# Two routed tiles of 128 rows moved into the last attention steps of a transformer block, with the order of output adds and weight transfers changed

## The chip, the cores and the metric

The kernel runs on one core of a Trainium2 chip. The metric is device time in microseconds (us). TensorE (PE) does the matmuls, VectorE (DVE) and ScalarE (ACT) the element-wise work, GpSimd (POOL) indirect transfers and some arithmetic, SyncE (SP) issues most transfers. Everything is in float32, where a matmul is done as two instructions on TensorE; 256 columns take 2 x 0.216 us.

## The reference

```python
x = x + attn(cond(x, cond_8, ...), ...)
x = x + ffn(cond2(x, cond_8, ...), ...)
# B, S, D = 4, 512, 256
# cond:  one of 8 gated MLPs (256 -> 512 -> 256) for each sequence, silu(up) * gate
# attn:  16 query heads of 16, one shared key/value head, softmax over 512 keys
# cond2: weights mixed from 8 matrices per sequence, masked: x @ w + bias
# ffn:   8 groups of 256 tokens, router with 8 experts, the top 2 chosen by each token,
#        at most 128 tokens of a group for one expert:
h = gelu_tanh(einsum('gech,ehf->gecf', expert_in, wi))     # 256 -> 1024
expert_out = einsum('gecf,efh->gech', h, wo)               # 1024 -> 256
out = einsum('gech,gtec->gth', expert_out, combine)        # combine = probability * dispatch
```

## The kernel before

**Attention.** There are 16 units (4 sequences of 4 units), each of 4 steps; a step is numbered n from -8 to 64 and has four slots i. In a slot the main loop emits the row maxima of eight steps ahead (`maxima`: a matmul into `pm`, L461, and a negated maximum on DVE, L463; none from step 56 on, since there is no unit left), the exponentials (`exponentials`: matmul `pe`, L490, and Exp on ACT, L491), and every second step the product of the weights e with v (`weigh`, 16 narrow matmuls L500 in slot 2). `shifts`, `shift_rows` (L480) carry a unit's maxima through DRAM back into the rows of `qq`.

**Side work.** All other work of the four sequences is cut into pieces. A track holds a list of pieces with a cost each, and a start and an end step; `pump(now)` runs pieces of the track that lags most, until what is due (at most 1100 cost units in a slot) is done. A piece emits matmuls into a bank from `side()`, a PSUM pool of two banks, and returns a `take`, the work on ACT or DVE that empties the bank, which `take_out` runs in the next slot; a take can return a second part for the slot after. A piece that returns OPEN keeps its bank for the next piece of its track. From step 38 (THIN) on, a slot without matmuls of a piece gets a filler, a matmul with zeros (`fill`, L516).

`finish(b)` holds the pieces after attention for sequence b: the output projection (L648), the transposes of r (L684), the mixing matmuls (L696), the router's choices on DVE and the scatter of the rows into `xp`, in one region per expert (`numbered`, L850, indirect transfers from GpSimd). Sequence 3's pieces run in the tail.

**Routed units.** After the rows of two sequences are scattered, the first full pairs of tiles (256 rows of one expert) are known. `full_list` lists them on DVE; `used` counts the pairs taken for each expert. The units are 3 "first", 4 "early" (listed after three sequences), 3 "pair", and 8 "last" with 320 to 96 rows. `fetch_in` and `fetch_out` bring a unit's weights (wi and wo, 1 MB each, three buffers of each) and rows. `up` multiplies (L1170) and applies the activation on ACT (L1174), `put` multiplies again (L1236), scales by the token's probability on DVE (`weights`, L1195 to L1213) and adds the rows to the output in DRAM by an indirect transfer with add (L1216), one for each tile of up to 128 rows. Unused rows point to spare output rows. The tail starts with `up` of the first unit, when the last attention step is emitted, and `go` interleaves up of unit t with put of unit t - 1; `pieces` lists what else is emitted at which chunk, a chunk being a fourth of a 256-row unit's up or put.

**Order of transfers.** SP's and GpSimd's queues run in the order written. The weights of the three first units are issued by GpSimd at steps (59, 2), (61, 1) and (62, 1). The reciprocals of the softmax sums of units 12 and 13 (`inverted`, the transfers `inv_rows<-hl`) are issued by SP at step 59 and used by `normalised` at (62, 1).

Of the kernel before, what the change touches and what calls it, by code (L numbers as in the profile page):

```python
# [32 lines left out]
NPAIR = NT // P  # L33
FIRST = 3
EARLY = 4
# [20 lines left out]
def adaln_attn_ffn_kernel(  # L56
# [154 lines left out]
    spare1 = numbers("spare1", [P, 1], [[0, 1]], NT + 1, 1)  # L211
# [40 lines left out]
    for n in range(4):  # L252
        t = apool.tile([P, 4, T], F32R, name=f"qq{n}")
        nc.gpsimd.memset(t[64:65].bitcast(F32), 0.0)
        qq.append(t)
# [17 lines left out]
    ep = attn_ctx.enter_context(tc.tile_pool(name="ep", bufs=2))  # L273
    scatters, last_rows, adds = [], [], []
# [603 lines left out]
    full_of = {"first": 2, "early": 3}  # L878
# [71 lines left out]

    used = lt("used", [P, NE])
    nc.gpsimd.memset(used, 0.0)

    def behind_used(first):
        nc.vector.scalar_tensor_tensor(
            first[:, 0:NE], used, 2.0 * P, first[:, 0:NE], ALU.mult, ALU.add
        )
        return first


    def full_list(name, n):
        whole = tiles_of(name, ALU.is_ge)

        nc.vector.tensor_scalar(whole, whole, -1.0, None, ALU.add)
        yield
        pairs = pairs_of(name, whole)
        nc.vector.tensor_tensor(pairs, pairs, used, ALU.subtract)
# [13 lines left out]
        nc.vector.tensor_tensor(used, used, end, ALU.add)  # L981
# [6 lines left out]
    def late_lists():  # L988
        count = lt("count", [P, NE])
        nc.vector.tensor_tensor(count, free, base[:, 0:NE], ALU.subtract)  # L990
        c = lt("c_more", [P, NE, 3])
# [4 lines left out]
        nc.vector.tensor_tensor(pairs, pairs, used, ALU.subtract)  # L996
        nc.vector.tensor_scalar(pairs, pairs, 0.0, None, ALU.max)
# [7 lines left out]
        whole = lt("whole", [P, NE])  # L1005
        nc.vector.tensor_tensor(whole, pairs, used, ALU.add)
        rest = lt("rest", [P, NE])
        nc.vector.scalar_tensor_tensor(rest, whole, -2.0 * P, count, ALU.mult, ALU.add)
        at = lt("at_rest", [P, NE])
        nc.vector.scalar_tensor_tensor(at, whole, 2.0 * P, base[:, 0:NE], ALU.mult, ALU.add)  # L1010
# [53 lines left out]
    def routed(units, alone=None):  # L1064
# [8 lines left out]
        def kind(t):  # L1073
            name, n = units[t]
            size = {"last": SIZES[n % NE], "rest": 2 * P + REST}.get(name, 2 * P)
            return lists[name], n, size
# [6 lines left out]
        def queue(t):  # L1083
            return nc.gpsimd if units[t][0] == "first" else nc.sync

        def fetch_in(t, weights=True, tokens=True):
# [23 lines left out]
            if name in full_of:  # L1110
                full = scatters[: 8 * full_of[name]]
                tc.declare_no_dep(
                    i.ins, group="rows", keep=[k.ins for k in full], reason="full tiles"
                )
                tc.add_to_no_dep_group(f"{name} rows", i.ins)
                if n == 0:
                    behind(i, full, "rows of the sequences so far")
            elif units[t] == ("pair", 0):
                behind(i, scatters, "rows of every sequence")

# [58 lines left out]


        def put(t):
            (expert, _), n, size = kind(t)
# [6 lines left out]
            def weights(i, m):  # L1189
                number, e0, p0, p1 = (  # L1190
                    xt_of[t][i][0:m, DX + j : DX + j + 1] for j in range(4)
                )
                w, v = w0[0:m, i : i + 1], w1[0:m, i : i + 1]
                te = expert[0:m, n : n + 1]
                nc.vector.scalar_tensor_tensor(w, e0, te, p0, ALU.is_equal, ALU.mult)  # L1195
                nc.vector.scalar_tensor_tensor(v, e0, te, p1, ALU.not_equal, ALU.mult)  # L1196
                nc.vector.tensor_tensor(w, w, v, ALU.add)
                nc.vector.scalar_tensor_tensor(v, number, 0.0, spare1[0:m], ALU.is_equal, ALU.mult)
                nc.vector.scalar_tensor_tensor(
                    at[0:m, i : i + 1], number, -1.0, v, ALU.add, ALU.add  # L1200
                )

            mine = []
            adds.append(mine)

            def out(i, m, p):
                weights(i, m)
                if m <= REST:
# [11 lines left out]
                    in_offset=None,  # L1220
                    compute_op=ALU.add,
# [3 lines left out]
                elif units[t] == ("pair", 0):  # L1225
                    behind(a, last_rows, "the last sequence's rows")
                mine.append(a)
# [22 lines left out]
            yield  # L1250

# [25 lines left out]
        return ahead, turned, go, turn, fetch_in  # L1277
# [28 lines left out]
    def pump(now):  # L1306
# [3 lines left out]
        due = min(sum(max(0, lag(t)) for t in tracks), 1100)  # L1310
        idle = True
        while due > 0 and any(t[4] for t in tracks):
# [3 lines left out]
            if t[4][0][1] in small_ones:  # L1316
                if now > THIN and loaded[0]:
# [46 lines left out]
    for b in range(B):  # L1364
# [3 lines left out]
        for g in range(NE):  # L1368
# [4 lines left out]
            shut.add((n, i))  # L1373
# [7 lines left out]
    ahead, turned, go, _, fetch_in = routed(units[:-1])  # L1381
    at(-4, 1, lambda: defer(router_bias()))
    first = list_parts(full_list("first", FIRST))
    for k in range(12):
        at(56 + k // 8, k // 2 % 4, first, 1)
    for t in range(FIRST):
        at(*((59, 2), (61, 1), (62, 1))[t], ahead, [t], True, False)
    at(58, 2, ahead, range(FIRST), False, True)
# [5 lines left out]
    for n in range(-LEAD, STEPS + 1):  # L1394
        m = n + LEAD
        for i in range(4):
# [23 lines left out]
            elif pump(n + (i + 1) / 4) or (n % 4, i) == (2, 1):  # L1420
                fill(n, i)
        if n == 36:
# [4 lines left out]
    for t in tracks:  # L1427
# [16 lines left out]
        3: [lambda: inverted(u)], 6: [lambda: fetch_in(FIRST)],  # L1444
# [10 lines left out]
    pieces[chunk + 5] = [lambda: late(99)]  # L1455
    chunks = 0
# [10 lines left out]
    last_ahead, _, last_go, last_turn, _ = routed(units[-1:], alone)  # L1467
# [5 lines left out]
    go(step, then, (FIRST,))  # L1473
# [4 lines left out]
    with tc.If(more > 0):  # L1478
        ahead, _, go, _, _ = routed(
# [83 lines left out]
```

## Time and profile before

| | |
|---|---|
| median of 3 runs | 654.77 us (653.52 to 658.9) |
| the profiled execution: time | 654.26 us |
| its span, first to last instruction | 652.6 us |
| mean granted clock of TensorE | 0.977 |
| PE busy in the span | 614.9 us (94%) |
| DVE, ACT, POOL busy | 340.5, 238.2, 175.8 us |
| moved by DMA | 97.37 MB |
| step 56's `weigh` starts, step 64's | 341.66, 380.83 us |
| the tail's first matmul | 382.69 us |

A chain of waits follows the work that ended last back through what released it. In its lines the first number is the start in us, the second the length. Windows give the busy time of each engine in a stretch; the last three columns are the granted clock of TensorE (1.00 is full), the share in which the DMA engines were busy, and GB/s.

### The profile page before, as it was taken

The numbers are of one execution on the slowest core, as the hardware profiler recorded it, in microseconds if no ns is written. First come the engines' busy times: TensorE is split into PE (matmuls) and PEld (weight loads), VectorE is DVE, ScalarE is ACT, GpSimd is POOL, SyncE is SP. The second block draws the span as 40 slices with busy tenths as digits, with TensorE's granted clock in tenths as the row PEclk, the third lists the DMA queues.
The fourth block names the chain that finished last, engine by engine and source line by source line (L and its number), as shares of the span: only waits on it lengthen the run. The fifth ranks groups of instructions, "written<-read, shape, count | busy, mean of one in ns | idle before, by whom it ended". The sixth has DMA issues, their size and how long they took to land.

```text
span 652.6 us, 8247 instructions
## 1 busy us (share of the span) xinstructions
PE 614.9 (94%) x2821; PEld 404.8 (62%) x2821; DVE 340.5 (52%) x913; ACT 238.2 (36%) x430; POOL 175.8 (27%) x182
## 2 busy tenths in 40 slices
PE   8999899999999999989998499999999999999991
PEld 3445454454455555655454258888889896878880
DVE  3269886668766668988877341247212112122420
ACT  2231556555655555555545341231121112121110
POOL 7008930049000100052024240124321211121231
PEclk9999999999999999999889799999999999999997
DMA  7297375658411242232217824656667777646221
GB/s 241 75 203 267 93 227 154 181 150 251 129 53 50 83 132 54 83 105 96 57 50 255 319 92 158 195 162 188 204 176 208 242 224 194 210 116 223 24 25 20
DMA packets 65876, 97.37 MB, mean 149 GB/s; under 512 B 8290, under 2 KB 37250, under 8 KB 65794
## 3 DMA queue, kind: packets, MB, share of 16 engines
q1 hardware_dynamic: 57826, 81.72, 40.6%
q0 software_dynamic: 8000, 15.04, 9.7%
q8 instruction: 25, 0.41, 0.3%
q14 instruction: 25, 0.20, 0.1%
HBM read 67.24 MB, written 29.24 MB: 148 GB/s over the span
## 4 chain that ended last, share of the span: by engine, by line
PE 79%; DMA 11%; DVE 4%; ACT 3%; issue 1%; POOLq 0%; SPq 0%; DVEq 0%
PE psA L1170 15%; PE psC L1236 14%; PE pa L500 9%; PE pm L461 9%; PE pe L490 9%; PE side L355 7%; DMA out_dram<-y,at 7%; PE side L339 4%; PE side L386 3%; DMA inv_rows<-hl 3%; PE side L648 2%; DVE negm L463 2%; PE side L696 2%; PE pa L516 2%; ACT e L491 2%
## 5 line engine op out<-in xcount | busy, mean ns | idle before, releaser
L491 ACT ACTIVATE e<-pe 128x512 f32<-128x512 f32 x256 | 147.7, 598 | 137.4 <-PE pe L490 133.0
L463 DVE TENSOR_REDUCE negm<-pm 128x1 f32<-128x512 f32 x256 | 167.9, 684 | 55.3 <-PE pm L461 55.0
L461 PE MATMUL pm<-kk,qq 65*128 65x512 f32 x256 | 148.3, 584 | 1.6 <-DVE negm L463 1.5
L1236 PE MATMUL psC<-wo_sb,hT 128*128 128x256 f32 (+2 forms) x544 | 115.4, 381 | 1.0 <-DVE xTr L1147 1.0
L490 PE MATMUL pe<-qq,kk 67*128 67x512 f32 x256 | 108.2, 428 | 2.7 <-ACT e L491 2.2
L1170 PE MATMUL psA<-xTr,wi_sb 128*128 128x256 f32 (+5 forms) x512 | 106.4, 365 | 0.9 <-ACT hT L1174 0.9
L1174 ACT ACTIVATE hT<-psA 128x512 f32<-128x512 f32 (+3 forms) x72 | 38.9, 544 | 183.3 <-PE psA L1170 183.3
L1236 PEld LDWEIGHTS psC<-wo_sb,hT 128*128 128x128 f32 (+2 forms) x544 | 93.2, 182 | 17.3 <-issue 1.7
L1216 POOL DMA_INDIRECT out_dram<-y,at x34 | 52.2, 1536 | 179.0 <-DVE w L1196 67.8
L1170 PEld LDWEIGHTS psA<-xTr,wi_sb 128*128 128x128 f32 x512 | 90.6, 191 | 14.5 <-issue 1.2
L461 PEld LDWEIGHTS pm<-kk,qq 65*128 65x128 f32 x256 | 49.3, 192 | 56.0 <-issue 21.1
L490 PEld LDWEIGHTS pe<-qq,kk 67*128 67x128 f32 x256 | 49.4, 193 | 36.1 <-ACT e L491 26.0
L500 PE MATMUL pa<-e,v 128*32 128x512 f32 x512 | 64.7, 625 | 0.0
L355 PE MATMUL side<-xT_sb,w 128*128 128x512 f32 x128 | 62.2, 595 | 2.2 <-DMA w<-in_wcond_dram 1.4
L1213 DVE TENSOR_SCALAR y<-psC,w 128x256 f32<-128x256 f32 (+1 forms) x30 | 14.4, 481 | 72.1 <-PE psC L1236 72.1
L850 POOL DMA_INDIRECT xp<-x,to_i x32 | 32.9, 1027 | 61.2 <-DVE negm L463 34.2
L1147 DVE COPY xTr<-psC 128x512 f32<-128x512 f32 (+5 forms) x18 | 10.5, 593 | 71.8 <-PE psC L1143 71.8
L577 POOL TENSOR_TENSOR x<-x,bo_sb 128x256 f32<-128x256 f32 x16 | 12.0, 767 | 116.7 <-DMA x<-in_xtok_dram 116.7
L355 PEld LDWEIGHTS side<-xT_sb,w 128*128 128x128 f32 x128 | 24.0, 190 | 18.3 <-issue 9.5
L500 PEld LDWEIGHTS pa<-e,v 128*32 128x32 f32 x512 | 13.9, 113 | 31.7 <-issue 31.1
L339 PE MATMUL side<-hid,w 128*128 128x512 f32 x64 | 31.7, 594 | 0.3 <-DVE hid L321 0.3
L313 DVE SCALAR_TENSOR_TENSOR u<-th,u 128x512 f32<-128x512 f32 x16 | 12.9, 809 | 21.1 <-ACT u L312 21.1
(274 smaller groups left out, 543.6 us busy)
## 6 DMA issues: line engine op xcount, KB each, us to landing
wi_sb<-in_wi_dram SPq DMA_DIRECT2D x14, 1024.0 KB
wo_sb<-in_wo_dram SPq DMA_DIRECT2D x14, 1024.0 KB
xp<-zeros SPq DMA_DIRECT2D x8, 1072.0 KB
qq<-qd SPq DMA_DIRECT2D x32, 256.0 KB
ov<-o SPq DMA_DIRECT2D x16, 256.0 KB
xt<-xp SPq DMA_DIRECT2D x15, 268.0 KB
w<-in_wcond_dram SPq DMA_DIRECT2D x12, 256.0 KB
wi_sb<-in_wi_dram POOLq DMA_DIRECT2D x3, 1024.0 KB, 9.4
```

The lines of the kernel that those rows point to most:

```text
L339: mm(po, wd[:, hc, ts(dc, P)], s["hid"][:, hc, :], start=hc == 0, stop=hc == 3)
L355: mm(s["ps"], s["w"][:, ds(first + P * c, P)], s["xT"][:, c, :], start=c == 0, stop=c == 1,)
L461: mm(pm, qq[u % 4][0:KMAX, hh, ts(i, P)], kk[0:KMAX, :], start=True, stop=True)
L463: nc.vector.tensor_reduce(negm[u % 2][:, c : c + 1], pm, AX.X, ALU.max, negate=True)
L490: mm(pe, kk[0:KEXP, ts(kc, P)], qq[u % 4][0:KEXP, i, :], start=True, stop=True)
L491: nc.scalar.activation(e_of[n][:, i, :], pe, AF.Exp)
L500: mm(pa_of[u][32 * i : 32 * i + 32, :], seqs[u // 4]["v"][:, kc, :], e[:, i], start=False, stop=kc == 3,)
L850: i = nc.gpsimd.indirect_dma_start(out=xp, out_offset=bass.IndirectOffsetOnAxis(ap=to_i[:, k, ch : ch + 1], axis=0), in_=s["x3"][:, ch, :] ...
L1170: mm(ph[:, f, :], of(wi_of[t], c * F + (first + f) * P, P), xT_of[t][:, c, 0:size], start=c == 0, stop=c == 1,)
L1174: nc.scalar.activation(hT_of[t][:, ds(first, per), 0:size], ph, AF.Gelu_apprx_tanh)
L1216: a = nc.gpsimd.indirect_dma_start(out=out_rows, out_offset=bass.IndirectOffsetOnAxis(ap=at[0:m, i : i + 1], axis=0), in_=y[0:m, i, :], in ...
L1236: mm(po[lo : lo + m, i % 2, :], hT_of[t][:, fc, ds(i * P, m)], of(wo_of[t], fc * D, D), start=fc == lo // REST, stop=fc >= F // P - (2 if ...
```

## The change

Two full tiles ("zero", of 128 rows each) are chosen by `zero_list` after the first sequence's rows are known, at steps 43 to 46. `used` counts tiles of 128 rows from now on, not pairs; the later lists subtract it. Their weights are brought by `part_in` in sixteen transfers of 256 KB, one every half step from (46, 2) to (54, 0), on GpSimd's queue. The computation is done by `beside`: nine pieces a tile, in tracks of steps 56 to 60 and 60 to 64. The activation is written out with Square and Tanh on ACT and two operations on DVE. EARLY is 3 instead of 4, so the tail has one unit of 256 rows less.

The adds of one unit's tiles are declared independent of each other and explicitly wait for the unit before; each tile index has spare output rows of its own. The first two units' weights are issued at (58, 0) and (61, 0), the third's by SP in chunk 4 of the tail; the first units' rows come at steps 58, 60 and 62 instead of all at 58. The fetch of unit 3 moves from chunk 6 to 8, the units after the early ones are fetched in two chunks of their own. Two of the four `qq` buffers are released after step 55 and give the space for `beside`'s tiles. From step 56 on `pump` no longer skips slots with weight mixing, and the limit of the router's small DVE pieces ends there.

```diff
-EARLY = 4
+EARLY = 3
+ZERO = 2
...
-spare1 = numbers("spare1", [P, 1], [[0, 1]], NT + 1, 1)
+spare1 = numbers("spare1", [P, 3], [[P, 3]], NT + 1, 1)
...
+    def zero_list():
+        whole = lt("tiles_first", [P, NE])
+        nc.vector.tensor_tensor(whole, free, begin[:, :, 1], ALU.is_ge)
+        yield
+        end = prefix("first", whole)
+        yield
...
+        nc.vector.tensor_reduce(expert, past, AX.X, ALU.add)
...
+        nc.vector.scalar_tensor_tensor(used, end, float(ZERO), whole, ALU.is_le, ALU.mult)
...
+        def part_in(t, k):
...
+            w, source = ((wi_of, wi), (wo_of, wo2))[k // 4]
+            queue(t).dma_start(
+                w[t][:, k % 4 : k % 4 + 1, 0:RUN],
+                source[ds(reg[t], P), ts(k % 4, RUN)].unsqueeze(1),
+            )
...
-            mine = []
+            mine, others = [], adds[-1] if t > 0 else []
+            same = f"unit {len(adds)}"
...
+                    bounds_check=NT + 3 * P - 1,
                     compute_op=ALU.add,
...
+                if mine:
+                    apart(a, same, "rows of one expert")
+                tc.add_to_no_dep_group(same, a.ins)
+                behind(a, others, "rows of other experts")
...
+        def beside(t, spare, cube, th):
...
+            def turned():
+                pt = side()
+                for c in range(2):
+                    nc.tensor.transpose(pt[:, ts(c, P)], xt_of[t][0][:, ts(c, P)], ident)
+                return lambda: nc.scalar.copy(xT.rearrange("p c t -> p (c t)"), pt[:, 0:D])
+
+            def up(first):
+                def piece():
+                    if first == 0:
+                        while pending:
+                            take_out()
+                    if first % 4 == 0:
+                        s["ps"] = side()
...
+                    for f in range(first, first + 2):
+                        for c in range(2):
+                            mm(
+                                ps[:, ts(f % 4, P)], of(wi_of[t], c * F + f * P, P), xT[:, c],
+                                start=c == 0, stop=c == 1,
+                            )
+
+                    def take():
+                        nc.scalar.activation(cube, ps, AF.Square, scale=0.044715**0.5)
+                        nc.vector.scalar_tensor_tensor(cube, cube, 1.0, ps, ALU.add, ALU.mult)
+                        return second
+
+                    def second():
+                        nc.scalar.activation(th, cube, AF.Tanh, scale=(2 / math.pi) ** 0.5)
+                        nc.vector.scalar_tensor_tensor(
+                            hT[:, ds(first - 2, 4), :].rearrange("p f t -> p (f t)"), th, 1.0, ps,
+                            ALU.add, ALU.mult,
+                        )
+                    return take if first % 4 else OPEN
...
+            def down(first):
...
+                    for fc in range(first, first + 2):
+                        mm(
+                            ps[:, 0:D], hT[:, fc, :], of(wo_of[t], fc * D, D),
+                            start=fc == 0, stop=fc == F // P - 1,
+                        )
...
+            return (
+                [(200, turned)] + [(1110, up(f)) for f in range(0, F // P, 2)]
+                + [(1070, down(f)) for f in range(0, F // P, 2)]
+            )
...
-    for t in range(FIRST):
-        at(*((59, 2), (61, 1), (62, 1))[t], ahead, [t], True, False)
-    at(58, 2, ahead, range(FIRST), False, True)
+    for t in range(FIRST):
+        if t < FIRST - 1:
+            at((58, 61)[t], 0, ahead, [t], True, False)
+        at(58 + 2 * t, 2, ahead, [t], False, True)
...
+            for t in range(ZERO):
+                track(56 + 4 * t, 60 + 4 * t, beside(t, spare, *two))
...
-        3: [lambda: inverted(u)], 6: [lambda: fetch_in(FIRST)],
+        3: [lambda: inverted(u)], 4: [lambda: ahead([FIRST - 1], True, False)],
+        8: [lambda: fetch_in(FIRST)],
...
+    for k in range(2):
+        pieces[chunk + 6 + k] = [lambda k=k: fetch_in(FIRST + EARLY + k)]
```

## The prediction

> **What bounds the kernel now.** I read the page first, then the chain of waits in order of time, then two-microsecond windows around the end of attention, and last the timeline of the final units.
>
> ```profile
> PE 614.9 (94%) x2821; PEld 404.8 (62%) x2821; DVE 340.5 (52%) x913; ACT 238.2 (36%) x430; POOL 175.8 (27%) x182
> PE 79%; DMA 11%; DVE 4%; ACT 3%; issue 1%; POOLq 0%; SPq 0%; DVEq 0%
> ```
>
> TensorE is nearly always busy, and most of the 11% of DMA on the chain lies in two places, as the chain in order of time shows (start, length):
>
> ```profile
> 351.24 1.86 PE pa L500 x16
> 355.21 17.98 DMA inv_rows<-hl
> 373.33 0.77 PE side L555
> ...
> 456.78 6.91 PE psA L1170 x32
> 464.12 6.92 PE psC L1236 x32
> 471.04 6.91 PE psA L1170 x32
> ...
> 600.15 39.13 DMA out_dram<-y,at
> ...
> 640.64 3.83 DMA out_dram<-y_alone,at_alone
> ```
>
> A unit of 256 rows in the tail is 6.91 + 6.92 us of matmuls and 0.4 of transposes: 471.04 - 456.78 = 14.26 us, and nothing but TensorE is between two units. Before the tail one small transfer, the reciprocals of the softmax sums, takes 18 us; at the end adds follow each other, each waiting for the one before. The windows (engine busy times, then granted clock, DMA share, GB/s) show what the first costs:
>
> ```profile
> 318.00:320.00 2.00, 1.82 (x9) 0.64 (x11) 1.93 (x8) 1.50 (x3) 0.00 (x0) 0.76 0.05 8
> 320.00:322.00 2.00, 2.00 (x16) 0.39 (x8) 1.21 (x4) 0.00 (x0) 0.00 (x0) 0.50 0.00 0
> ...
> 364.00:366.00 2.00, 1.64 (x12) 1.27 (x10) 0.90 (x6) 1.37 (x4) 0.00 (x0) 1.00 1.04 386
> 366.00:368.00 2.00, 0.00 (x0) 0.00 (x0) 0.00 (x0) 0.45 (x2) 0.00 (x0) 0.71 1.03 390
> ...
> 374.00:376.00 2.00, 2.00 (x11) 0.65 (x14) 1.02 (x2) 0.60 (x1) 0.00 (x0) 0.50 0.00 0
> ```
>
> The DMA engines are full from 353 to 372 us with 6 MB of weights from GpSimd's queue; TensorE stands still for 7.58 us and then runs at half clock until about 377.
>
> **Part 1, a unit leaves the tail.** EARLY falls from 4 to 3, so one unit of 14.26 us goes: **-14.3 us**. Its 256 rows come back as two tiles of 128 in steps 56 to 64. Nothing in the tail becomes late by it as far as I see: the pair list is ready at 449.5 us and the first pair's rows landed about 465 against a need at about 464 then, but the scatters in front (450.4 to 460) start some 3 us earlier when the add ahead of them no longer waits. Bounds: -14.3 to -12.
>
> **Part 2, adds of a unit apart.** The end today:
>
> ```profile
> 631.34 7.08 PE L1236 MATMUL psC<-wo_sb_alone,hT_alone 128*128 128x256 f32 x32
> 638.46 0.48 DVE L1213 TENSOR_SCALAR y_alone<-psC,w_alone 96x256 f32<-96x256 f32 x1 [2.15 <-PE psC L1236]
> 640.64 1.56 POOL L1216 DMA_INDIRECT out_dram<-y_alone,at_alone  x1 [4.30 <-issue]
> 645.25 1.44 POOL L1216 DMA_INDIRECT out_dram<-y_alone,at_alone  x1 [3.05 <-DMA out_dram<-y_alone,at_alone]
> ```
>
> The last rows are ready at 638.94, their add starts at 645.25, because the first add of the unit waited for the unit before and the second for the first. One add takes about 5 us (1.55 of issue, 3 to 4 until it lands), and the last units bring two or three per 11 to 15 us, so only this part of the tail is held by adds. Apart, a unit of three takes 3 x 1.55 + 4 = 8.7 us, less than its matmuls; the last add starts at 639.0: **-6.2 us**. Two adds in flight may land later: bounds -6.3 to -3. The bounds_check operand is not shown on an add; the scatter that has one is issued in 1.03 us against 1.54, so I take 0, with -0.5 to +0.5 in the last add.
>
> **Part 3, the new list.** About nine DVE operations of 0.16 to 0.22 us (rows L896 to L917) in steps 43 to 46, where DVE is full (windows of 1.00 at 289 to 295 us) and its negm reductions release TensorE: **+1.6 us** (0 to 2). The sixteen small weight transfers of 256 KB come out half a step apart on GpSimd's queue, which idles there; 0.25 MB per 2.2 us is a third of the 380 GB/s that the rows of 354 to 372 us show, and the transfers that steps 48 to 55 need are issued two steps ahead. I take 0 (0 to 2).
>
> **Part 4, steps 56 to 64.** From the first product of weights and values in step 56 (341.66) to that of step 64 (380.83) is 39.2 us now: 7.6 of standstill, some 1.7 lost to half clock after it, and 29.9 of the rest. The third unit's weights go behind the tail's start; the first two units' transfers start at steps 58 and 61, the reciprocals between them at step 59 and needed at 62: about 3 MB at 380 GB/s is 8 us, less than two of the longer steps. So the standstill goes (-9.3).
>
> In its place comes work. Per tile: two transposes 0.25, up with 128 columns 3.6 (the 128-row unit at 499.35 takes 3.57), down 16 x 0.216 = 3.5; two tiles **+14.6 us**. Free TensorE time for it is little: 14 filler matmuls L516 of 0.215 us lie in the stretch, and the order by due times replaces about ten: **-2.1**.
>
> Then waits. A half of the up product (one PSUM bank) is freed only after Square, DVE, Tanh, DVE: by ACT's 0.60 (L491), DVE's 0.75 to 0.81 (L321, L313) twice each, with an exponential of 0.60 queued ahead, 3.4 us. There are two banks for all side work, so the next but one user stands in TensorE's queue, and the exponentials' matmuls behind it. Following the due times slot by slot, the users behind the four halves are the transposes of r in step 57, the third mix of 57, the second half of tile 1 in 61, and the places of 61. Matmuls between cover some of each; at the second-last the routed weights and L500's 1.86 us cover most. The same row today, with one copy in the chain instead of four links:
>
> ```profile
> 344.08 1.32 PE L684 MATMUL side<-ident,r 128*128 128x128 f32 x8
> 346.16 1.20 PE L696 MATMUL side<-wb,rT 128*128 128x264 f32 x4 [0.75 <-ACT rT L685]
> 347.43 0.39 PE L516 MATMUL pa<-zeros 128*128 128x512 bf16 x1
> ```
>
> I take 2.5 + 2 + 0.5 + 2 = **+7 us** (0 if the pieces cover each other, 13 if each costs all of 3.4), and +1.4 for the copy of the transposed rows ahead of the first up piece, before the stretch begins. Square is not in the trace; Copy, Identity, Tanh and Exp follow each other without a table load, so I take none; a load is 1.28 us (L1174), and two around each of four Squares would be 10 us.
>
> **Clock.** The windows at 318 to 322 show half clock after only 0.2 us of idle in the two microseconds before, with narrow matmuls of 65 rows; the 0.75 us wait at 346 led to none. One half-speed window of 3.4 us loses up to 1.7 us. I take one: **+1.7** (0 to 8.5, one after each of five waits).
> The Trainium skill (TensorE: Matmul & The Clock Gate, Part 1: The HAM clock gate) has the clock halve after at least one idle window of about 3.4 us. By that rule waits of 2 to 3 us would cost nothing more, and the sum would be 1.7 us lower; the row at 318 us disagrees, so I keep the 1.7.
>
> Stage: 29.9 + 14.6 - 2.1 + 7 + 1.4 + 1.7 = 52.5 against 39.2, **+13.3 us**.
>
> **One queue more.** Step 58 now puts 2 MB just ahead of the small transfer (L480) that brings unit 15's shift rows, due in step 60. Before, the same order held by chance (348.61 and 349.50), and the exponentials at 357.81 waited for ACT alone. I take 0.
> A rule speaks against this order: the Trainium skill (DMA: Bandwidth & Descriptors, Queues, rings and completion order) says that a transfer's semaphore lands only after every earlier write of its DMA engine, across queues. That fits the 18 us of the reciprocals; for the shift rows the row of before shows no wait within two steps, and by the rule at most the drain of 3 MB would count.
>
> **Sum.** -14.3 - 6.2 + 1.6 + 13.3 = -5.6 us; +0.9 for the third unit's 2 MB beside the last reciprocals at the tail's start (0 to 3, needed some 8 us after its issue). The profiled execution took 654.26 us (span 652.6 and 1.7 around it), close to the median of 654.77: 654.26 - 4.7 = **649.6 us**. All low ends: stage 29.9 + 14.6 - 3 = 41.5 (+2.3), -14.3 - 6.2: 636. All high ends: stage 29.9 + 14.6 + 13 + 1.4 + 8.5 = 67.4 (+28.2), -12 - 3 + 2 + 3 and 2 for the small transfers: 674.
>
> **Rivals.**
> *The steps swallow the pieces.* For it: ACT is busy 0.5 to 0.95 of the windows there, TensorE has fillers, waits of ACT and pieces may overlap, and waits shrink to 2 us in all. Against: fillers are only 3 us. Stage 29.9 + 14.6 - 3 + 2 = 43.5 (+4.3): -14.3 - 6.2 + 1.6 + 4.3 = -14.6, **639.7 us**. Chance 0.25.
> *The two banks and the clock (slower).* Every half costs TensorE the full 3.4 us, 13.6 in all, and each of the four waits and the one for the copy drops the clock for a window, 5 x 1.7 = 8.5: stage 29.9 + 14.6 - 2.1 + 13.6 + 1.4 + 8.5 = 65.9 (+26.7), so -14.3 - 6.2 + 1.6 + 26.7 + 0.9 = +8.7, **663 us**. For it: all side work has two banks, and the row at 318 us shows how little idle time halves the clock. Against: from 340 to 366 us waits of 0.75 and 1.0 us left the clock at 1.00. It decides from a stage of about 57 us. Chance 0.18.
> *The adds do not come apart*, the last one still waiting for the unit's first: 649.6 + 5 = **654.6 us**. For it: the last unit is built by a separate call of routed, and only the queue's records of before, not the text, show which wait an add has. Chance 0.10.
> The forecast keeps 0.47, its own range 644 to 655.
>
> **How the numbers follow.** A measurement of this kernel tells about 1% from no change, 6.5 us. Faster by over 1% (below 648.2) is the first rival and 0.17 of the forecast's 0.47: 0.42. Same is the forecast's other 0.30 and the adds' 0.10: 0.40. Slower 0.18. The range 638 to 663 leaves 1 in 10 on each side.
>
> **What would show it.** Right: no 18 us hl on the chain; weights-and-values products of steps 56 and 64 some 50 us apart, with TensorE waiting for DVE before L684 and L696; the tail one unit shorter; the last add under 1 us after its y. Wrong: that distance near 43 (first rival) or over 57 with the clock at 0.5 in several windows (second), or a wait of the last add for a landing (third).

## The result, and the profile after

The changed kernel took **662.66 us** (median of 4 runs, 661.72 to 663.84) against 654.14 us for the kernel before, measured beside it: a ratio of **1.0134, 95% interval 1.0092 to 1.0175**. The forecast was 649.6 us and faster; the kernel became slower. (The ratios here leave out disturbed executions, which the medians keep, so the two can differ by up to 1%.)

The page's first line, which before showed PE at 614.9 us and 2821 matmuls:

```profile
PE 619.3 (94%) x2844; PEld 410.5 (62%) x2844; DVE 344.9 (52%) x925; ACT 241.8 (37%) x436; POOL 183.3 (28%) x195
```

The share stays at 94% while the span grows from 652.6 to 661.5 us. A table by stage says more. It is read from the timeline of TensorE: the starts of the weights-and-values products (L500 before, L504 after) of steps 50, 56 and 64, the tail's first matmul, the end of the last one, and the span's end. "Again" is the same changed kernel in a later group of runs (a0 below).

| stage, us | before | after | after, again |
|---|---|---|---|
| to step 50 | 311.35 | 312.15 | 310.92 |
| step 50 to 56 | 30.31 | 36.42 | 36.46 |
| step 56 to 64 | 39.17 | 55.50 | 53.66 |
| step 64 to the tail | 1.86 | 1.86 | 1.85 |
| tail | 255.73 | 246.88 | 241.52 |
| last matmul to the end | 14.2 | 8.7 | 8.7 |
| span | 652.6 | 661.5 | 653.1 |

The two last stages gave back what was forecast (the tail in "again" at least); the stage of the side tiles is a little longer than forecast; and the stage ahead of it lost 6.1 us, where the prediction had only the copy for the first tile (1.4 us, which it counted in the side tiles' stage). By steps: 50 to 52 lost 7.5 us (15.5 against 8.0), 52 to 54 gained 3.1, since the kernel before runs there in part at half clock, and 54 to 56 lost 1.7, with the first tile's transposes, copy and first matmuls in them. The windows (engine busy times, granted clock, DMA share, GB/s) show the loss of steps 50 to 52 first:

```profile
318.00:320.00 2.00, 0.00 (x0) 0.00 (x0) 0.00 (x0) 0.44 (x1) 0.31 (x1) 0.84 0.82 231
320.00:322.00 2.00, 0.00 (x0) 0.00 (x0) 0.89 (x4) 0.00 (x0) 0.00 (x0) 0.50 0.89 258
322.00:324.00 2.00, 0.80 (x1) 0.29 (x1) 1.97 (x6) 0.00 (x0) 0.00 (x0) 0.50 0.60 153
...
354.00:356.00 2.00, 0.00 (x0) 0.00 (x0) 1.62 (x7) 1.25 (x3) 0.34 (x1) 1.00 0.75 176
...
358.00:360.00 2.00, 2.00 (x8) 1.72 (x7) 1.09 (x2) 0.60 (x1) 0.00 (x0) 0.50 1.03 408
```

TensorE does nothing from 317.5 to 322.5 us, while the DMA engines move 230 to 260 GB/s. The timeline after, by engine, says with what (start, length, engine, line, operation, and in brackets the idle time before it and what ended it):

```profile
302.74 1.09 POOL L1155 DMA_DIRECT2D wi_sb<-in_wi_dram  x2
303.81 2.12 POOL L1155 DMA_DIRECT2D wo_sb<-in_wo_dram  x4
305.92 2.27 POOL L1155 DMA_DIRECT2D wi_sb<-in_wi_dram  x4
...
308.25 0.34 SPq L531 DMA_DIRECT2D ov<-o  x1
316.49 0.64 SPq L537 DMA_DIRECT2D sm<-ov  x1
321.05 0.35 DVE L544 RECIPROCAL sm<-sm 128x32 f32<-128x32 f32 x1 [4.66 <-DMA sm<-ov]
322.50 0.80 PE L465 MATMUL pm<-kk,qq 65*128 65x512 f32 x1 [4.97 <-DVE negm L467]
325.02 0.77 PE L494 MATMUL pe<-qq,kk 67*128 67x512 f32 x1 [1.73 <-DMA qq<-md]
```

Twelve of the sixteen weight parts (3 MB) leave GpSimd's queue between 300.15 and 308.2 us, ten of them without a pause, not half a step (2.2 us) apart; the last four follow at 315.99 us. The results of a unit, the attention sums among them, go to memory with ov<-o (256 KB), and a later transfer of SP, sm<-ov (16 KB), reads the sums back when that has landed. It is issued 8.2 us after ov<-o, where before it was 2.0 us:

```profile
307.47 0.34 SPq L527 DMA_DIRECT2D ov<-o  x1
309.50 0.63 SPq L533 DMA_DIRECT2D sm<-ov  x1
```

VectorE then stands in its queue in front of the reciprocals for 4.66 us, its negm reductions behind them, and TensorE behind those. Right after it TensorE waits another 1.73 us, for a unit's shift rows (qq<-md); in f1 and g4 below this second wait is the longer one (5.05 and 4.29 us).

The waits of TensorE in steps 56 to 64, and the one just ahead of them:

```profile
347.14 1.16 PE L1323 MATMUL side<-xT_beside,wi_sb 128*128 128x128 f32 x8 [0.95 <-ACT xT_beside L1311]
356.15 0.66 PE L688 MATMUL side<-ident,r 128*128 128x128 f32 x4 [3.66 <-ACT rT L689]
365.40 1.13 PE L700 MATMUL side<-wb,rT 128*128 128x264 f32 x4 [2.48 <-DVE hT_beside L1335]
376.44 0.50 PE L494 MATMUL pe<-qq,kk 67*128 67x512 f32 x1 [1.16 <-ACT e L495]
377.88 2.08 PE L1323 MATMUL side<-xT_beside,wi_sb 128*128 128x128 f32 x8 [0.73 <-ACT xT_beside L1311]
390.84 0.19 PE L801 MATMUL side<-prev,ones_b 128*128 128x64 bf16 x1 [1.74 <-DVE prev L786]
```

10.7 us in all. The 3.66, 2.48 and 1.74 us stand at three of the four users of the banks that the prediction named (L688 and L700 are L684 and L696 of before, L801 is in the places), and 0.95 us is the copy; the fourth, the second half of tile 1, shows no wait. There is no 18 us hl any more. The clock is at 0.5 behind the waits at 356, 377 and 391 us.

The end, with no add waiting for a landing:

```profile
652.85 0.48 DVE L1251 TENSOR_SCALAR y_alone<-psC,w_alone 96x256 f32<-96x256 f32 x1 [2.16 <-PE psC L1280]
653.61 1.44 POOL L1254 DMA_INDIRECT out_dram<-y_alone,at_alone  x1 [1.38 <-DVE y_alone L1251]
```

And one stall in the tail's second unit that this execution alone shows:

```profile
417.08 1.08 ACT L1213 ACTIVATE hT<-psA 128x512 f32<-128x512 f32 x2 [5.21 <-remote]
418.09 4.08 PE L1209 MATMUL psA<-xTr,wi_sb 128*128 128x256 f32 x10 [4.55 <-ACT hT L1213]
```

TensorE, ScalarE and VectorE all stand still there from 413.5 to about 417 us, and for the last two the trace names no instruction and no transfer of the kernel that released them ("remote"). In every later profile TensorE's wait is 0.90 us, as before (391.20 us there).

### The profile page after: what moved, and what is told of

Read it like the earlier page. It is cut to its first block, busy times and chain, and to the rows that moved or that the text cites. A ratio compares the mean times of both kernels' runs of the same rounds, so it can differ in the third digit from the quotient of the medians.

```text
span 661.5 us, 8411 instructions
## 1 busy us (share of the span) xinstructions
PE 619.3 (94%) x2844; PEld 410.5 (62%) x2844; DVE 344.9 (52%) x925; ACT 241.8 (37%) x436; POOL 183.3 (28%) x195
## 5 line engine op out<-in xcount | busy, mean ns | idle before, releaser
L465 PE MATMUL pm<-kk,qq 65*128 65x512 f32 x256 | 147.8, 583 | 6.5 <-DVE negm L467 6.5
L494 PE MATMUL pe<-qq,kk 67*128 67x512 f32 x256 | 110.9, 435 | 4.0 <-ACT e L495 1.9
L1280 PE MATMUL psC<-wo_sb,hT 128*128 128x256 f32 (+2 forms) x512 | 108.3, 381 | 1.0 <-DVE xTr L1186 1.0
L1209 PE MATMUL psA<-xTr,wi_sb 128*128 128x256 f32 (+5 forms) x480 | 101.1, 368 | 4.6 <-ACT hT L1213 4.6
L1213 ACT ACTIVATE hT<-psA 128x512 f32<-128x512 f32 (+3 forms) x68 | 36.5, 540 | 176.7 <-PE psA L1209 166.2
L1280 PEld LDWEIGHTS psC<-wo_sb,hT 128*128 128x128 f32 (+2 forms) x512 | 86.9, 181 | 16.7 <-issue 1.7
L1209 PEld LDWEIGHTS psA<-xTr,wi_sb 128*128 128x128 f32 x480 | 85.6, 193 | 18.0 <-ACT hT L1213 4.8
L1254 POOL DMA_INDIRECT out_dram<-y,at x32 | 49.1, 1536 | 161.9 <-DVE w L1224 137.6
L465 PEld LDWEIGHTS pm<-kk,qq 65*128 65x128 f32 x256 | 49.2, 192 | 59.2 <-DVE negm L467 22.6
L504 PE MATMUL pa<-e,v 128*32 128x512 f32 x512 | 64.4, 623 | 0.0
L504 PEld LDWEIGHTS pa<-e,v 128*32 128x32 f32 x512 | 13.8, 113 | 32.2 <-issue 31.7
```

The lines of the kernel that those rows point to most:

```text
L465: mm(pm, qq[u % 4][0:KMAX, hh, ts(i, P)], kk[0:KMAX, :], start=True, stop=True)
L494: mm(pe, kk[0:KEXP, ts(kc, P)], qq[u % 4][0:KEXP, i, :], start=True, stop=True)
L504: mm(pa_of[u][32 * i : 32 * i + 32, :], seqs[u // 4]["v"][:, kc, :], e[:, i], start=False, stop=kc == 3,)
L1209: mm(ph[:, f, :], of(wi_of[t], c * F + (first + f) * P, P), xT_of[t][:, c, 0:size], start=c == 0, stop=c == 1,)
L1213: nc.scalar.activation(hT_of[t][:, ds(first, per), 0:size], ph, AF.Gelu_apprx_tanh)
L1254: a = nc.gpsimd.indirect_dma_start(out=out_rows, out_offset=bass.IndirectOffsetOnAxis(ap=at[0:m, i : i + 1], axis=0), in_=y[0:m, i, :], in ...
```

## The experiments

Each group ran on one chip beside its own runs of the kernel before: medians of before 647.87 (e1 to e4), 650.46 (a0, e5 to e7), 649.32 (f1 to f4) and 649.56 us (g1, g3, g4). For the second group only medians are compared. The theory: two separate losses eat the gain, the transfers of the attention sums behind 3 MB of weights in steps 50 to 52, and in steps 56 to 64 the waits for the two banks with half clock behind them. The rivals: that ScalarE's and VectorE's own work (the new list among it) holds these stages, that the third unit's weights only moved their stall into the tail, and that the low clock has other reasons than idle time. The change of `pump` and the released qq buffers were not run alone.

**e1, adds apart alone** (on the kernel before):

```diff
-    spare1 = numbers("spare1", [P, 1], [[0, 1]], NT + 1, 1)
+    spare1 = numbers("spare1", [P, 3], [[P, 3]], NT + 1, 1)
...
+                if mine:
+                    apart(a, same, "rows of one expert")
+                tc.add_to_no_dep_group(same, a.ins)
+                behind(a, others, "rows of other experts")
```

> The kernel before with one part of the change alone: the adds of one unit go out without waiting for each other. Theory (two banks and clock; this part did what was forecast): the time from the last matmul to the end of the span falls from 14.2 us to about 8.7 as in the changed kernel, everything before stays, so about 5.5 us faster than before (648.7 against 654.1). Rival (the shorter end in the changed kernel comes from its other order of units, not from the adds): under 1.5 us faster.

Median 644.14 us; ratio 0.9884 (0.9816 to 0.9952). The trace is nearly that of before up to the last matmul (637.99 us against 638.42); then:

```profile
638.02 0.48 DVE L1216 TENSOR_SCALAR y_alone<-psC,w_alone 96x256 f32<-96x256 f32 x1 [2.15 <-PE psC L1244]
638.78 1.44 POOL L1219 DMA_INDIRECT out_dram<-y_alone,at_alone  x1 [1.38 <-DVE y_alone L1216]
```

The last add starts 0.28 us after its rows (645.25 before). From the last matmul to the end it is 8.1 us instead of 14.2: this part is worth 6.1 us by itself in the trace, which lies within the interval of the ratio (3 to 12 us).

**e2, the third unit's weights later, alone:**

```diff
-        at(*((59, 2), (61, 1), (62, 1))[t], ahead, [t], True, False)
+        if t < FIRST - 1:
+            at(*((59, 2), (61, 1))[t], ahead, [t], True, False)
...
-        3: [lambda: inverted(u)], 6: [lambda: fetch_in(FIRST)],
+        3: [lambda: inverted(u)], 4: [lambda: ahead([FIRST - 1], True, False)],
+        8: [lambda: fetch_in(FIRST)],
```

> The kernel before with only the third unit's 2 MB of weights moved from step 62 to behind the tail's start. Theory: the 7.6 us standstill at the reciprocals of step 62 is a transfer behind 6 MB of weights, so it shrinks with 4 MB in front of it; the products of steps 56 and 64 come 31 to 34 us apart instead of 39.2, and the kernel is 5 to 8 us faster than before. Rival (the saved standstill is given back at the tail's start, where the changed kernel shows a stall of 4.6 us while the third unit's weights land): the standstill goes, but the tail's start shows a stall of about 4 us, and the gain is 1 to 4 us.

Median 645.89; ratio 1.0013 (0.9971 to 1.0055): no difference shown, and the theory's 5 to 8 us lie outside the interval. Steps 56 to 64 took 35.1 us, 4.1 less, and the tail 256.1, no worse:

```profile
369.18 0.77 PE L555 MATMUL side<-inv_rows,spread 128*128 128x512 f32 x1 [2.73 <-DMA inv_rows<-hl]
```

The standstill went from 7.58 to 2.73 us, not to 0: 2 MB less is 4.85 us less, about what 2 MB take at 380 GB/s (5.5 us). They did not stand in front of the reciprocals' transfer: in the kernel before this was issued at 354.38 us, the weights of the three units at 348.61, 355.44 and 361.18 us, so that two of the three lay behind it. The rival's stall at the tail's start isn't there.

**e3, other banks** (on the changed kernel; pmx holds the three banks of the maxima, which end with step 55):

```diff
+            def own_bank():
+                return pmx.tile([P, T], F32, name="pm")
...
-                pt = side()
+                pt = own_bank()
...
-                        s["ps"] = side()
+                        s["ps"] = own_bank()
```

> The changed kernel with the side tiles' sums in three other PSUM banks that are idle by step 56, in place of the two that all side work shares. Theory (the two banks and the clock): the waits of 3.66, 2.48 and 1.74 us in front of the transposes of r, of the next side work and of the places go, and with them most of the half clock behind them (16.7 us at half speed); steps 56 to 64 shrink from 55.5 us to 43 to 47, so 8 to 12 us faster than the changed kernel, about 652. Rival (the steps are held by the work of ScalarE and VectorE, and the banks only show it): the stage stays at 52 to 56 us, under 3 us faster.

Median 646.20; ratio to before 0.9987 (0.9959 to 1.0015), where the changed kernel is at 1.0154 (f4). The stage took 43.1 us, within the theory's 43 to 47, at full clock throughout, with waits of 2.15 (the copy of the transposed r, now ahead of the first mix) and 1.52 us left. The stall at 317 us is still there: 6.97 us ahead of a matmul L465.

**e4, the weight parts held:**

```diff
-        nc.scalar.activation(e_of[n][:, i, :], pe, AF.Exp)
+        paced_by[:] = [nc.scalar.activation(e_of[n][:, i, :], pe, AF.Exp)]
...
+            behind(i, paced_by, "not ahead of its slot")
```

> The changed kernel with each of the sixteen small weight transfers held until the exponential of its own half step, so that they can't be issued in a row. Theory (3 MB issued within 8 us and the small transfers behind them stop TensorE at 317 to 322 us): the stall of 5.0 us and the 1.7 us behind it go, step 50 to 52 falls from 15.5 us to 8 to 10, and the kernel is 4 to 6 us faster than the changed one, about 657. Rival (that stall comes from the new list's work on VectorE, not from transfers): step 50 to 52 stays at 14 to 15.5 us, under 1.5 us faster.

Steps 50 to 52 took 9.3 us instead of 15.5, and sm<-ov follows ov<-o after 2.0 us again:

```profile
306.80 0.34 SPq L532 DMA_DIRECT2D ov<-o  x1
308.83 0.64 SPq L538 DMA_DIRECT2D sm<-ov  x1
```

So the stall comes from the transfers, not from the new list. It is not quite gone: TensorE still waits 1.48 us for the shift rows (2.4 to 2.7 us in e5, f2 and g3 below). The time hardly followed: median 653.61, ratio 1.0124 (1.0081 to 1.0168). The profiled execution was the fastest of six (648.87 at a clock of 0.982); the others took 652.8 to 655.8 at 0.972 to 0.977. Even in the fastest the clock halved behind all four places of waits in steps 57 to 62, the 2.48 us included. What holding the parts is worth was left open here.

**a0, the changed kernel again,** and in more rounds **f4:**

> The changed kernel once more, as the measure for the two behind it. Theory: the stall at 317 to 322 us, the three waits of steps 57 to 62 and some 16 us at half clock in steps 56 to 64 come again, since the order of the work makes them; the stall of 4.6 us in the tail's first unit, which neither the run with other banks nor the one with the held weights showed, may be of that one execution. If it was, the kernel takes 4 to 5 us less than then against before (ratio 1.006 rather than 1.013); if the stall is here again, it belongs to the order and the ratio stays near 1.013.

> The changed kernel in more rounds on the same chip as the three others, as their measure. Theory: slower than before by 0.6 to 1.0%, the stall at 317 to 322 us and the three waits again, no stall in the tail's first unit. Rival (the stall there is part of the kernel and comes in most executions): 1.3% slower, with the wait of 4.6 us in the trace.

a0: 654.56 against 650.46 us. f4: median 656.36 against 649.32, ratio 1.0154 (1.0104 to 1.0204). In both profiles the stall at 317 us is back (4.94 and 4.71 us), and the waits of steps 57 to 62 (stage 52.7 us in f4); the wait in the tail is 0.90 us. So the 4.55 us were not in every execution. Span times clock is 641.6 to 643.1 us in the four first executions and 637.6 to 638.7 in the eleven of a0 and f4, which fits the stall in all of the former and in none of the latter; only three of the fifteen were traced, and why it came stays open. But f4's ratio is no smaller than the first one (by the medians 1.011 against 1.013), so the rest of the losses carries the verdict.

**e5, banks and held parts together:**

> The changed kernel with both edits: other banks for the side tiles, and each weight transfer held until its own half step. Theory (two separate losses): steps 50 to 52 take 8 to 10 us and steps 56 to 64 take 43 to 46, the tail starts at 385 to 390 us, the span is 634 to 640, 1.0 to 1.5% under the kernel before. Rival (what one edit saves, the other's stall takes back, as the time of the run with held weights suggests): the tail starts at 394 or later and the time is within 0.5% of the run with other banks alone.

Median 642.82 us in 4 runs (650.46 before): 640.75 to 644.23, and one, the profiled, at 650.02, with 17 us lost to half clock there and 7 to 10 in the others. The profiled one missed the theory's stages (steps 50 to 52 took 11.4 us, steps 56 to 64 47.7), and its tail began at 398.6 us, as the rival had it, with the clock at half in between; the median is 1.2% under before, as the theory had it.

**e6 and f1, the waits filled.** The waiting instructions stay where they are, but TensorE multiplies zeros ahead of them. In e6 only the middle group of zeros reached its wait: the helper issues none in the first slots of a unit, and the third group was written for the places of sequence 3 instead of 2. So e6 decided nothing: 653.52 us, stage 52.7. f1 puts all three into an idle bank:

```diff
+    def kept_busy(k):
+        pz = pmx.tile([P, T], F32, name="pm")
+        for _ in range(k):
+            mm(pz, zeros_b[:, 0:P], zeros_b, start=True, stop=True)
...
+                if b == 2 and c == 1:
+                    kept_busy(13)
...
+                if b == 2 and n == 2:
+                    kept_busy(11)
...
+            if b == 2:
+                kept_busy(8)
```

> The changed kernel with matmuls of zeros put in front of three of the waiting instructions of steps 57 to 62: 16 ahead of the second transposes of r, 11 ahead of the third mix, 8 between the two sums of the places, 0.215 us each, 7.5 us in all. The waits stay as long as they are, with TensorE busy in them. Theory (idle time lowers the clock, and half of what the stage loses is clock): the half clock behind those waits goes, the stage shrinks from 55.5 us to 48 to 52, 4 to 7 us faster than the changed kernel. Rival (the low clock there isn't due to idle time): the stage stays or gets longer by the matmuls that do not fit into the waits.

> The changed kernel with matmuls of zeros into an idle bank in front of the three long waits of steps 57 to 62 (13 ahead of the second transposes of r, 11 ahead of the third mix, 8 between the sums of the places, 0.215 us each, 6.9 us in all). In the run before, only the 11 ahead of the mix were really issued: the helper leaves out a unit's first slot. Theory (half of what the stage loses is clock, and idle time lowers it): the three waits shrink below 0.5 us each, the half clock behind them goes, the stage shrinks from 53.7 to 46 to 50 us, 3 to 6 us faster than the changed kernel. Rival (the clock there isn't set by idle time): half clock stays, under 1 us or a loss.

f1: median 651.01, ratio 1.0048 (1.0016 to 1.0079), 5.4 us under f4's median on the same chip. The stage took 47.9 us. Windows of a0, which has the waits, first (after the busy times the clock, DMA share, GB/s):

```profile
352.00:356.00 4.00, 2.10 (x7) 1.56 (x8) 2.02 (x7) 1.69 (x3) 1.16 (x2) 0.67 0.77 276
356.00:360.00 4.00, 4.00 (x16) 3.60 (x16) 1.09 (x2) 1.07 (x2) 0.00 (x0) 0.50 1.08 371
...
388.00:392.00 4.00, 2.57 (x9) 1.59 (x8) 2.63 (x13) 1.74 (x4) 0.00 (x0) 0.86 0.00 1
392.00:396.00 4.00, 4.00 (x22) 1.29 (x22) 1.02 (x2) 1.09 (x2) 0.00 (x0) 0.71 0.01 4
```

and of f1:

```profile
352.00:356.00 4.00, 3.77 (x19) 2.15 (x18) 2.04 (x8) 1.69 (x3) 1.18 (x2) 1.00 0.82 263
356.00:360.00 4.00, 4.00 (x27) 3.23 (x26) 1.49 (x3) 2.28 (x4) 0.00 (x0) 1.00 1.06 375
...
388.00:392.00 4.00, 4.00 (x28) 2.31 (x28) 1.78 (x7) 1.79 (x3) 0.00 (x0) 1.00 0.00 0
392.00:396.00 4.00, 4.00 (x27) 2.89 (x30) 2.06 (x12) 1.85 (x4) 1.45 (x1) 1.00 0.00 0
```

From 356 to 360 us TensorE is fully busy in both, but gets through 27 matmuls instead of 16 (not all of one size). The fillers do no work; they hold the clock. That is 53.7 - 47.9 = 5.8 us of the stage by a0, and 52.7 - 47.9 = 4.8 by f4. Span times clock is 637.9 to 639.4 us in f1's runs and 637.6 to 638.1 in f4's, so the whole gain is clock.

**f2, everything taken out; e7 and f3, no side tiles at all.** f2 is e5 with 9 and 8 such fillers ahead of the two waits that e3 left. e7 and f3 are one kernel: e1 and e2 together, on the kernel before, so without the new list, the weight parts and the side tiles.

> The changed kernel with other banks and held weight transfers (as e5) and with matmuls of zeros ahead of the two waits that are left (9 ahead of the first mix of steps 56 to 60, 8 between the sums of the places). Theory: at full clock the stage is about 43 us, and it stays there in every execution; the time is 639 to 642 us, 1.2 to 1.7% under before. Rival (fillers only lengthen the queue): the same time as e5, 642 to 645.

> The kernel before with the adds apart and the third unit's weights behind the tail's start, without the side tiles. Theory: the sum of both alone, 6.0 us at the end (last add under 1 us after its rows) and 4 us between steps 56 and 64; span some 10 us shorter than before, ratio 0.984 to 0.988. Rival (with the adds apart, what is saved ahead of the tail is lost in it): ratio 0.99 or more.

> The kernel before with the adds apart and the third unit's weights behind the tail's start, no side tiles, in more rounds. Theory (two tiles in the steps cost TensorE as much as the unit that leaves the tail): it equals or beats the changed kernel with all its stalls taken out (f2) within 0.5%, at a ratio of 0.983 to 0.988 to before. Rival (the steps swallow part of the tiles' work once the stalls are gone): f2 is faster than this one by 3 us or more.

f2: median 643.89, ratio 0.9974 (0.9941 to 1.0007), stage 43.1 us at full clock. f3: 642.06, ratio 0.9936 (0.9904 to 0.9969); e7: 639.72 against 650.46. f3's median is 1.8 us below f2's on the same chip, which is not clear of noise; so with most stalls gone the side tiles bring nothing that shows. One wait for a transfer is left in each: 2.52 us for the shift rows in f2 (at 321.6 us), 3.29 us for the reciprocals in f3. Both ratios are 0.6 to 1.4% nearer to 1 than was expected of them.

**g1, the second unit's weights held too** (on f3's kernel):

```diff
+                if (name, n) == ("first", 1):
+                    behind(i, paced_by, "not ahead of its slot")
```

> The kernel before with the adds apart, the third unit's weights behind the tail's start, and the second unit's 2 MB held until the exponentials of step 61, so that they can't go out just behind the reciprocals' small transfer. Theory (the rest of the standstill, 3.3 us in the run of two parts, is the second 2 MB, issued 0.8 us after the small transfer at 354 us): no standstill at the reciprocals, steps 56 to 64 take 31 to 32 us instead of 35, span 3 to 5 us shorter than with the two parts alone, ratio to before 0.984 to 0.990. Rival (the standstill is the first 2 MB's, or the saved time comes back as a wait for the second unit's weights): the wait stays, or the tail's second unit waits for wi_sb, and the ratio is 0.992 or more.

```profile
350.49 1.50 SPq L546 DMA_DIRECT2D inv_rows<-hl  x2
360.12 0.76 POOL L1096 DMA_DIRECT2D wi_sb<-in_wi_dram  x1 [9.25 <-ACT e L492]
```

In f3 these weights went out 0.8 us after the reciprocals (354.07 and 354.90), and TensorE waited 3.29 us for the reciprocals; here they go out 9.6 us later and no wait is left. Steps 56 to 64 took 29.6 us. Median **637.63 us against 649.56, ratio 0.9895 (0.9823 to 0.9966)**: the lowest median of all these kernels, though the intervals of e1, f3 and g1 overlap.

**g3 and g4, the price of the weight parts at an undisturbed clock.** g3 is f1 with the parts held as in e4; g4 is f1 again.

> The changed kernel with fillers ahead of the three bank waits (as f1) and each of the sixteen small weight transfers held until its own half step (as e4). It prices the transfers' stall at a clock that the waits no longer disturb. Theory (the stall of steps 50 to 52 is worth 5 to 6 us): 4 to 6 us faster than f1 on the same chip, 645 to 647, ratio to before about 0.997. Rival (half of the stall comes back elsewhere, as the time of e4 suggests): under 2.5 us faster than f1.

> The changed kernel with the fillers ahead of the three bank waits once more, as the measure for g3 on the same chip. Theory: as before, 651 us, ratio 1.003 to 1.006 to before, full clock from 340 to 400 us. Rival (the full clock there was one execution's luck): half clock in that stretch and 654 us or more.

g3: median 647.05, ratio 1.0038 (0.9987 to 1.0090); g4: 650.83, ratio 1.0086 (1.0048 to 1.0125). The difference of the medians is 3.8 us, between the two expectations. The intervals of the ratios overlap; put beside each other, the twelve runs of each differ by 3.5 us in the mean, give or take 1.7. g4's stage took 49.5 us, with the clock at 0.72 to 0.85 between 372 and 380 us behind the two waits that f1 does not fill; f1's own profile had been spared that. In g3's profile the clock fell between 320 and 340 us all the same. That is where the 5 us of e4 may have gone in part: the time that the stall took is partly time that the kernel without it loses to half clock there, as the kernel before does (its steps 50 to 56 took 30.3 us, those of e7 and g1, with the clock at 1.00, 25.5).

## Why the prediction was wrong, point by point

| term | forecast, us | measured, us | from |
|---|---|---|---|
| a unit leaves the tail | -14.3 | -14.2 (-8.9 in the first profile, with the stall of 4.6) | tail of a0, after |
| adds apart | -6.2 | -6.1 alone, -5.5 in the changed kernel | e1, after |
| new list | +1.6 | -0.4 to +0.8, up to step 50 | a0, after |
| sixteen weight parts | 0 (0 to 2) | +7.5 in steps 50 to 52, +6.1 in steps 50 to 56; 3.8 in the time | after; g3, g4 |
| standstill | -9.3 | gone in the changed kernel; the third unit's weights alone give -4.1 | after, e2 |
| tiles, less fillers, with the copy | 14.6 - 2.1 + 1.4 = 13.9 | 43.1 - 29.9 = 13.2, some 3.7 of it waits filled with zeros; 1.7 more in steps 54 to 56 | f2; after |
| waits for the banks | +7 | 47.9 - 43.1 = 4.8 (idle at the three places 6.8) | f1, f2 (a0) |
| half clock behind them | +1.7 | 53.7 - 47.9 = 5.8; by f4 52.7 - 47.9 = 4.8; by g4 53.7 - 49.5 = 4.2 | a0, f1, f4, g4 |
| third weights beside the last reciprocals | +0.9 | +0.3 | tail of e2 |

**The step that failed is the sixteen transfers**, "half a step apart on GpSimd's queue", taken at 0. In the first profile the span grew by 8.9 us where 4.7 less was forecast; of these 13.6 us, 6.1 came in steps 50 to 56, 4.5 in the tail (its stall and the half clock behind it) and 3.0 in steps 56 to 64. In a0, without that stall, the miss is 5.2 us, and steps 50 to 52 alone lost 6.6. The slots of the program say when an instruction is written, not when its engine comes to it. GpSimd had nothing to wait for (the weight buffers were free), so its queue ran ahead, and 3 MB stood on the DMA engines when the sums' transfers came. The prediction compared rates (a third of 380 GB/s) where it should have asked what each issue waits for. It had both halves at hand, since its first section explained the 18 us of hl by 6 MB of weights on the DMA engines, and Part 3 named the transfers that steps 48 to 55 need. It even had a rule for it: the Trainium skill (DMA: Bandwidth & Descriptors, Queues, rings and completion order) has a transfer's semaphore land behind every earlier write of its DMA engine across queues. That was weighed for step 58 alone, not for steps 46 to 55. Here 3 MB in front stretched 2.0 to 8.2 us, which fits the rule, though no run tells it from transfers that only share the engines. The 18 us of the reciprocals, which the prediction found to fit it, do so only in part: the 2 MB that e2 and g1 took away had been issued 6.8 and 0.8 us behind that small transfer, and the wait fell by 4.85 and 3.29 us. So transfers issued later on another queue delayed it too.

**The stage came out nearly as forecast, by errors that cancelled:** 52.7 us in f4, 53.7 in a0 and 55.5 at first against 52.5. The tiles' cost came out near, three of the four bank waits stood where the due times had put them and were by f1 and f2 2.2 us too dear, and **the clock was mis-sized**, 1.7 for 4.2 to 5.8 us. One half-speed window was taken; in a0 the waits of 2.59 us (at 353.9), of 1.16 and 0.73 us (at 375.4 and 376.8) and of 1.74 us (at 389.1) each brought one or more, and that of 2.48 us (at 364.4) none, though in e4 it did. The weighing against the Trainium skill (TensorE: Matmul & The Clock Gate, Part 1: The HAM clock gate) went the right way: no wait of a0 in that stage reaches 3.4 us, and the clock halved three times.

**What was right:** the tail's unit, the adds, and that the tiles in the steps cost about what the unit in the tail did (13.2 and 1.7 against 14.2), so that the gain had to come from the adds and the standstill. f3 and f2 show this from the other side.

**The rivals.** The slower one, 663 us, had the mechanism of the stage, but not its sizes (its stage was 65.9), and met the first number by luck. The measured 55.5 lies below its deciding point of 57; the rest of the way came from the transfers and from the tail's stall, which it didn't have. The forecast's test for the second rival (over 57 with low clock in several windows) was half met. "The steps swallow the pieces" fell: f2 gets to 43.1 us, near its 43.5, but only with other banks. The adds came apart.

**Against which execution.** a0's span is only 0.5 us over the profiled one of before, yet its median lies 4 us above. The profile of before was an execution at 0.977, with 15.0 us lost (span times one minus clock), 5 of them around 318 to 331 us. Over f4's group the executions of before lose 11.7 us that way in the median and those of the changed kernel 17.0: 5.3 of the 7.0 us between the medians.

## What to carry to other kernels

A slot in the program paces a transfer only if its issue has something to wait for at that time; otherwise the engine's queue runs ahead and bulk transfers pile up in front of small ones that the compute waits for. Bulk issued just behind a small one delays it as well. Tie each bulk issue to an instruction of its slot, late enough for the small one to have landed (e4: the sums after 2.0 us again; g1: no wait left). Work moved beside a full TensorE saves only what TensorE idles there; ask first which idle time it fills, then which buffers it shares, and expect a wait to cost more than its idle time, since half clock can follow it.

## What the runs showed of the hardware that was not expected

Filling waits with useless matmuls made this kernel faster: 6.9 us of zeros gave 5.4 us in the median (f1, f4), since the clock was held up: in f1's profile it is 1.00 from 340 to 396 us.

A transfer of 16 KB was delayed by bulk transfers issued after it from another engine's queue: without the 2 MB issued 6.8 us behind it TensorE waited 4.85 us less (e2), and without those issued 0.8 us behind it the remaining 3.29 us went (g1).

Whether a short idle time halves the clock differs from one execution to the next. The kernel before fell to 0.76 and 0.50 in the windows from 318 to 322 us with TensorE busy 1.80, 1.82 and 2.00 us of each two from 316 on. e7 has the same order there and the same busy times:

```profile
316.00:318.00 2.00, 1.80 (x7) 0.75 (x5) 1.97 (x6) 1.95 (x4) 0.00 (x0) 1.00 0.10 16
318.00:320.00 2.00, 1.82 (x16) 0.84 (x19) 1.93 (x9) 1.27 (x3) 0.00 (x0) 1.00 0.00 0
320.00:322.00 2.00, 2.00 (x18) 0.99 (x9) 1.59 (x4) 0.37 (x1) 0.00 (x0) 1.00 0.02 5
```

and e3 kept 1.00 through waits of 2.15 and 1.52 us. The wait of 2.48 us left it at 1.00 in a0 and f4 and brought 0.50 in e4 (from 358 us). So a single profile can't price a wait of that size; the clock listed with every run can. For e4's six runs the span times the clock is 635.5 to 636.2 us while the spans reach from 647.3 to 654.1: all that spread is clock. The Trainium skill (TensorE: Matmul & The Clock Gate, Part 1: The HAM clock gate) has the activity window run free, so that its phase differs from run to run; that would fit, but no run here tests it.
